# One-hot matrices built tile by tile from a scalar per edge, and counts by two products a pair, in a graph network kernel

## The chip, the cores and the metric

The kernel runs on one core of one Trainium2 chip. The metric is the time of one execution on the device in microseconds (us), the median of several runs; less is better. A core has five engines with an instruction queue each: TensorE (PE in the profile, its weight loads PEld), VectorE (DVE), ScalarE (ACT), GpSimd (POOL) and SyncE (SP, which only issues transfers here). All share a scratch memory of 128 partitions (SBUF); TensorE writes its results to PSUM.

## The reference

A graph network of three layers over 6250 nodes with 256 features and 100,000 edges of three types (relations). Edges are sorted by their target `dst`. Cut to what matters:

```
ew = edge_attr @ edge_w + edge_b                       # 100000 x 256
rel_masks = [(edge_type == i) for i in range(3)]
inv_cnt = [1 / max(segment_sum(m, dst), 1) for m in rel_masks]
for l in range(3):
    msg = relu(x[src] * ew)                            # a gather of 100000 rows
    out = 0
    for i in range(3):
        h = segment_sum(msg * rel_masks[i], dst) * inv_cnt[i]
        out += h @ weights[l, i]
    x = x + relu(out + x @ roots[l] + biases[l])
return layernorm(x_in + x)
```

All tensors are float32.

## The kernel before

The edges are cut into tiles of 128, one edge to a partition; two tiles make a *pair* (391 pairs), two pairs a *q* of four tiles. The layers' loop body `layer` walks through the pairs in a fixed `order` that is written out by hand (the scheduler is off: what the Python code says first stands first in each engine's queue). In step `it` of a layer it does the following.

- `gather` (line 900, in `gather_pair`) fetches the rows `x[src]` for the pair nine steps ahead: two indirect transfers on POOL's queue, one for each tile, each with 128 rows of 1 KB, into the tile `xs`. Behind the two stands `breath` (line 904): POOL fills 512 columns of a tile that nobody reads with zeros, a rest for the queue. The tiles `xs` of eight q can be in flight. The first six pairs of the next layer are gathered early, behind the last of this one.
- `reduce` (lines 641 to 647) makes the segment sums of the step's pair on TensorE: the rows `xs` as weights, the one-hot matrices `oh` as the moving side, two halves of the features by two tiles, each pair of products summed in PSUM (`h_p`).
- `make_ew` computes the edge weights `ew_p` in PSUM (lines 602 and 606), `add` (line 659) adds `h_p` to the running sums `acc` at a place that VectorE reads from a register.
- `weigh`, for the q three steps ahead, multiplies the rows by `ew_p` on VectorE (line 627) and takes Relu on ScalarE (line 629). VectorE waits here for the gathered rows to land.
- The node part: `root_turn` to `root_keep` (lines 664 to 677) and `node_mul`, `node_end` (lines 687 to 721) finish a chunk of 128 nodes every few steps, and write it to `x_mid`, from which the next layer gathers; the last layer's `norm` is line 738.
- `one_hot`, for the q two steps ahead, builds the matrices. Each edge has a number `seg` = 40 x type + distance of its target from the first target of its pair, and its row of the one-hot is 1 at that column of 120 (`WK`). One VectorE instruction (line 634) compares all four tiles: the counting row `iota_w` and `seg`, both stretched to 128 x 4 x 120.

In layer 0 alone the edges of each node and type are counted too. `one_hot` adds the two one-hots of a pair and rounds to bfloat16 (`oh_b`, line 638, VectorE), and `reduce` multiplies the sum by a matrix of ones (`full_ones`, line 647): one product a pair, into a third part of `h_p` (`CH` is 3 in layer 0 and 2 later; `DC` is 2).

A table `came` of comparisons with a scalar per partition is built once in layer 0 (line 568), by twelve instructions.

Of the kernel before, what the change touches and what calls it, by code (L numbers as in the profile page):

```python
# [9 lines left out]
BF = mybir.dt.bfloat16  # L10
I32 = mybir.dt.int32
AF = mybir.ActivationFunctionType
ALU = mybir.AluOpType
# [429 lines left out]
def ordered_path(ctx, tc, x, attr_laid, A, weights, roots, biases, edge_w, edge_b, out, src, src_i, seg, place_i, consts, x_root,  # L443
# [6 lines left out]
    nc = tc.nc  # L450
    P = 128
# [8 lines left out]
    DC = D // P  # L460
    WK = R * WIN
# [10 lines left out]
    ident, ones, iota_w = consts  # L472
# [40 lines left out]
    full_ones = big.tile([P, P], BF, name="full_ones")  # L513
# [15 lines left out]
    edge = ctx.enter_context(tc.tile_pool(name="edge", bufs=2))  # L529
# [40 lines left out]
    def layer(l, r_sb, b_sb, ats, early, pools):  # L570
# [7 lines left out]
        CH = DC + 1 if l == 0 else DC  # L578
        xs, ew_ps, ohs, h_ps, o_ps, rs = {}, {}, {}, {}, {}, {}
        x0s, mvs, oh_bs, t_ss, places = {}, {}, {}, {}, []  # L580
# [11 lines left out]
        def pairs_of(q):  # L592
            return range(min(2, U - 2 * q))
# [37 lines left out]
        def one_hot(q):  # L631
            ohs[q] = edge.tile([P, 4, WK], F32, name="oh", bufs=3)
            n = 2 * len(pairs_of(q))
            nc.vector.tensor_tensor(ohs[q][:, :n, :], iota_w[:, None, :].to_broadcast([P, n, WK]),  # L634
                                    seg[:, 4 * q:4 * q + n, None].to_broadcast([P, n, WK]), op=ALU.is_equal)
            if l == 0:
                oh_bs[q] = edge.tile([P, 2, WK], BF, name="oh_b", bufs=3)
                nc.vector.tensor_tensor(oh_bs[q][:, :n // 2], ohs[q][:, 0:n:2], ohs[q][:, 1:n:2], op=ALU.add)  # L638

        def reduce(u):  # L640
            h_ps[u] = h_pool.tile([P, DC + 1, WK], F32, name="h_p")
            for d in range(DC):
                for i in range(2):
                    nc.tensor.matmul(h_ps[u][:, d, :], xs[u // 2][:, u % 2, i, d * P:(d + 1) * P],  # L644
                                     ohs[u // 2][:, u % 2 * 2 + i, :], start=(i == 0), stop=(i == 1))
            if l == 0:
                nc.tensor.matmul(h_ps[u][:, DC, :], full_ones, oh_bs[u // 2][:, u % 2, :], start=True, stop=True)  # L647

        def add(u):
            if places[:1] != [u // 8]:  # L650
# [109 lines left out]
        for it in range(-11, max(starts) + 7):  # L760
# [21 lines left out]
            if pair(0) is not None:  # L782
                reduce(pair(0))
# [39 lines left out]
            if pair(2) is not None and first_of(it + 2, 2):  # L823
                one_hot(pair(2) // 2)
# [242 lines left out]
```

## Time and profile before

| | us |
|---|---|
| median of 3 runs | 3532.93 |
| lowest, highest | 3525.73, 3533.65 |
| the profiled execution | 3533.41 |
| its span in the profile | 3531.5 |

The span runs from the first instruction to the last. The mean granted TensorE clock was 0.86 of full speed. A group's row in the profile gives the line, the engine, the operation, the tile written and those read, the shapes, the number of instructions, then the time that the group was busy in us and the mean of one in ns, then the idle time of the engine just before them and what ended it ("issue" is a gap that no wait explains). A row of a line's own view gives the shortest, median and longest duration in ns. A row of the timeline gives the start and the duration in us, the engine, the line and, in brackets, the idle time before it. A row of the waits gives who waited for whom, the total in us, the times, and the longest.

### The profile page before, as it was taken

Reading aid. Unit: us, or ns where it says so; the run is one execution under the profiler, and the core shown is the slowest. Engines: PE = TensorE matmul, PEld = TensorE weight load, DVE = VectorE, ACT = ScalarE, POOL = GpSimd, SP = SyncE. Lnnn points to the kernel's source line nnn. Section 1 sums busy time; section 2 is a strip of 40 time slices with the busy share of each in tenths; the row PEclk is TensorE's granted clock in tenths of the full one; section 3 lists DMA queues with packets and bytes.
Section 4 is the critical chain, followed back from the end, with each engine's and each line's share of the span. In section 5 each row is a group of like instructions: output and inputs, shape, how many; then the busy total and the mean of one; then the engine's idle time right before and its main releaser. Section 6 shows DMA issues by size and latency. Waiting matters only on the chain.

```text
span 3531.5 us, 53355 instructions
## 1 busy us (share of the span) xinstructions
PE 2670.8 (76%) x18484; PEld 2212.9 (63%) x18484; DVE 2061.2 (58%) x4306; ACT 816.9 (23%) x959; POOL 2950.6 (84%) x3522
## 2 busy tenths in 40 slices
PE   5777777877787777777777777677787787777776
PEld 4666666666666566666666666556666666666655
DVE  6666666666765545555555555445555565666644
ACT  2222222222221122222222222112222222222221
POOL 7888888888888788888888888888888888888886
PEclk9888889998987888888889888778888888889877
DMA  5343433333333333333333333333334334333332
GB/s 161 107 119 115 124 106 106 108 106 111 112 111 106 106 102 102 103 105 107 104 108 107 110 111 113 106 105 111 115 113 115 107 112 115 113 109 111 111 100 82
DMA packets 173312, 387.75 MB, mean 110 GB/s; under 512 B 43418, under 2 KB 78636, under 8 KB 173036
## 3 DMA queue, kind: packets, MB, share of 16 engines
q0 software_dynamic: 112608, 307.65, 30.6%
q1 hardware_dynamic: 53136, 68.50, 6.2%
q10 hardware_dynamic: 7292, 8.11, 0.7%
q8 instruction: 151, 2.47, 0.3%
q14 instruction: 125, 1.02, 0.1%
HBM read 364.62 MB, written 19.46 MB: 109 GB/s over the span
## 4 chain that ended last, share of the span: by engine, by line
POOL 55%; issue 16%; PE 16%; DVE 6%; DMA 5%; POOLq 1%; ACT 0%; DVEq 0%; another core or an unknown queue 0%; ACTq 0%
POOL xs L900 43%; POOL breath L904 11%; PE h_p L644 7%; PE o_p L687 3%; DMA xs<-x_mid,src_io 3%; DVE xs L627 3%; PE ew_p L606 2%; DMA xs<-in_x_dram,src_io 1%; DVE acc L659 1%; PE r_p L672 1%; PE ew_p L602 1%; DVE x_root L718 1%; DVE oh L634 1%; POOLq L900 0%; PE h_p L647 0%
## 5 line engine op out<-in xcount | busy, mean ns | idle before, releaser
L900 POOL DMA_INDIRECT xs<-x_mid,src_io x1564 | 1544.9, 988 | 375.4 <-issue 359.0
L644 PE MATMUL h_p<-oh,xs 128*128 128x120 f32 x9336 | 1437.4, 308 | 350.7 <-DVE acc L659 230.4
L644 PEld LDWEIGHTS h_p<-oh,xs 128*128 128x128 f32 x9336 | 1335.8, 218 | 532.5 <-DVE acc L659 286.4
L627 DVE TENSOR_TENSOR xs<-ew_p,xs 128x512 f32<-128x512 f32 x1167 | 789.6, 687 | 1235.2 <-DMA xs<-x_mid,src_io 875.6
L629 ACT ACTIVATE xs<-xs 128x1024 f32<-128x1024 f32 (+1 forms) x588 | 617.7, 1051 | 2629.9 <-DVE xs L627 2369.1
L900 POOL DMA_INDIRECT xs<-in_x_dram,src_io x770 | 760.2, 987 | 180.9 <-issue 175.8
L904 POOL MEMSET breath<- 128x512 f32 x1167 | 634.8, 544 | 0.6
L659 DVE TENSOR_TENSOR acc<-h_p,acc 128x240 f32 (+1 forms) x1173 | 519.0, 442 | 108.6 <-PE o_p L687 30.4
L687 PE MATMUL o_p<-w_sb,acc 128*128 128x256 f32 (+1 forms) x1716 | 511.0, 441 | 76.4 <-DVE x_root L718 45.8
L606 PEld LDWEIGHTS ew_p<-ew_sb,at 32*128 32x128 f32 x4692 | 304.0, 225 | 319.3 <-issue 310.6
L602 PE MATMUL ew_p<-bias,full_ones 3*128 3x512 bf16 x1173 | 228.1, 419 | 329.4 <-DVE xs L627 274.9
L687 PEld LDWEIGHTS o_p<-w_sb,acc 128*128 128x128 f32 (+1 forms) x1716 | 355.4, 220 | 166.0 <-issue 39.4
L606 PE MATMUL ew_p<-ew_sb,at 32*128 32x256 f32 x4692 | 438.6, 469 | 3.7 <-issue 3.7
L634 DVE TENSOR_TENSOR oh<-iota_w,seg_o 128x480 f32<-128x480 f32 x588 | 381.2, 648 | 0.0
L672 PE MATMUL r_p<-r_sb,t_s 128*128 128x256 f32 x588 | 202.1, 477 | 76.6 <-ACT t_s L668 64.7
L718 DVE SCALAR_TENSOR_TENSOR x_root<-o_p,inv,x_root 128x256 f32<-128x256 f32 (+1 forms) x429 | 205.8, 480 | 34.3 <-PE o_p L687 15.5
L672 PEld LDWEIGHTS r_p<-r_sb,t_s 128*128 128x128 f32 x588 | 127.6, 241 | 101.0 <-ACT t_s L668 69.2
L704 ACT ACTIVATE acc<-zero_o 128x768 f32<-128x768 f32 (+1 forms) x150 | 140.3, 935 | 37.5 <-PE r_p L687 23.7
L602 PEld LDWEIGHTS <-full_ones 3*128 3x128 bf16 x1173 | 34.1, 92 | 139.1 <-issue 107.4
L647 PE MATMUL h_p<-oh_b,full_ones 128*128 128x120 bf16 x391 | 89.6, 229 | 0.1
L638 DVE TENSOR_TENSOR oh_b<-oh 128x240 bf16<-128x240 f32 x196 | 80.2, 409 | 6.7
L675 DVE TENSOR_TENSOR x_root<-r_p,b_sb 128x256 f32<-128x256 f32 x147 | 61.2, 416 | 8.6 <-PE r_p L672 2.7
(93 smaller groups left out, 564.0 us busy)
## 6 DMA issues: line engine op xcount, KB each, us to landing
at<-in_attr_laid_dram SPq DMA_DIRECT2D x147, 256.0 KB
xs<-x_mid,src_io POOLq DMA_INDIRECT x1564
xs<-in_x_dram,src_io POOLq DMA_INDIRECT x770
x_mid<-x_all SPq DMA_DIRECT2D x96, 128.0 KB
x_all<-in_x_dram ACTq DMA_DIRECT2D x8, 768.0 KB
x<-in_x_dram SPq DMA_DIRECT2D x48, 128.0 KB
out_dram<-x_all SPq DMA_DIRECT2D x48, 128.0 KB
w_sb<-in_L_gnn_weights_dram SPq DMA_DIRECT2D x3, 768.0 KB
```

Of the source, the lines that this page charges most:

```text
L602: nc.tensor.matmul(banks[j].rearrange("p i d -> p (i d)"), full_ones[j * A:j * A + PARTS, :], bias[j * A:j * A + PARTS].rearrange("p i d - ...
L606: nc.tensor.matmul(banks[j][:, i, :], ats[OCT * o // GROUP][j * A:(j + 1) * A, o % (GROUP // OCT), i, :], ew_sb[j * A:(j + 1) * A, :], sta ...
L627: nc.vector.tensor_mul(xs[q][:, k], ew_ps[2 * q + k], xs[q][:, k])
L629: nc.scalar.activation(there, there, AF.Relu)
L634: nc.vector.tensor_tensor(ohs[q][:, :n, :], iota_w[:, None, :].to_broadcast([P, n, WK]), seg[:, 4 * q:4 * q + n, None].to_broadcast([P, n, ...
L644: nc.tensor.matmul(h_ps[u][:, d, :], xs[u // 2][:, u % 2, i, d * P:(d + 1) * P], ohs[u // 2][:, u % 2 * 2 + i, :], start=(i == 0), stop=(i ...
L659: nc.vector.tensor_tensor(there, h_ps[u][:, :CH].rearrange("p c (r w) -> p c r w", r=R), there, op=ALU.add)
L672: nc.tensor.matmul(rs[c][:, 1, :], t_ss[c][:, d, :], r_sb[:, d, :], start=(d == 0), stop=(d == DC - 1))
L687: nc.tensor.matmul(o_p[:n, j, :], acc[:, d, r, slot:slot + n], w_sb[:, r * DC + d, :], start=(d == 0), stop=(d == DC - 1))
L718: nc.vector.scalar_tensor_tensor(root, o_p[:n, j, :], inv[:n, c, r:r + 1], root, op0=ALU.mult, op1=ALU.add)
L900: nc.gpsimd.indirect_dma_start(out=xs[:, u % 2, i, :], out_offset=None, in_=x_rows[:, :], in_offset=bass.IndirectOffsetOnAxis(ap=src_i[:, ...
L904: nc.gpsimd.memset(breath, 0.0)
```

## The change

`one_hot` no longer compares four tiles in one instruction with two stretched tensors. It issues one `tensor_scalar` for each tile: the row `iota_w` compared with one scalar per partition, the tile's column of `seg`. In layer 0 the four one-hots of a q are no longer summed by pairs on VectorE; ScalarE copies all four to bfloat16 (`oh_b` has four tiles now), and `reduce` counts by two products a pair with the matrix of ones, summed in PSUM as the others are. The gathers and `breath` stay as they are.

```diff
         def one_hot(q):
             ohs[q] = edge.tile([P, 4, WK], F32, name="oh", bufs=3)
             n = 2 * len(pairs_of(q))
-            nc.vector.tensor_tensor(ohs[q][:, :n, :], iota_w[:, None, :].to_broadcast([P, n, WK]),
-                                    seg[:, 4 * q:4 * q + n, None].to_broadcast([P, n, WK]), op=ALU.is_equal)
+            for t in range(n):
+                nc.vector.tensor_scalar(ohs[q][:, t, :], iota_w, seg[:, 4 * q + t:4 * q + t + 1], None,
+                                        op0=ALU.is_equal)
             if l == 0:
-                oh_bs[q] = edge.tile([P, 2, WK], BF, name="oh_b", bufs=3)
-                nc.vector.tensor_tensor(oh_bs[q][:, :n // 2], ohs[q][:, 0:n:2], ohs[q][:, 1:n:2], op=ALU.add)
+                oh_bs[q] = edge.tile([P, 4, WK], BF, name="oh_b", bufs=3)
+                nc.scalar.activation(oh_bs[q][:, :n], ohs[q][:, :n], AF.Copy)
 
         def reduce(u):
             h_ps[u] = h_pool.tile([P, DC + 1, WK], F32, name="h_p")
-            for d in range(DC):
+            for d in range(CH):
                 for i in range(2):
-                    nc.tensor.matmul(h_ps[u][:, d, :], xs[u // 2][:, u % 2, i, d * P:(d + 1) * P],
-                                     ohs[u // 2][:, u % 2 * 2 + i, :], start=(i == 0), stop=(i == 1))
-            if l == 0:
-                nc.tensor.matmul(h_ps[u][:, DC, :], full_ones, oh_bs[u // 2][:, u % 2, :], start=True, stop=True)
+                    nc.tensor.matmul(h_ps[u][:, d, :],
+                                     xs[u // 2][:, u % 2, i, d * P:(d + 1) * P] if d < DC else full_ones,
+                                     (ohs if d < DC else oh_bs)[u // 2][:, u % 2 * 2 + i, :],
+                                     start=(i == 0), stop=(i == 1))
```

## The prediction

> **What bounds the kernel now.** I read the page first: busy times, the chain that ended last, and the groups of POOL.
>
> ```profile
> PE 2670.8 (76%) x18484; PEld 2212.9 (63%) x18484; DVE 2061.2 (58%) x4306; ACT 816.9 (23%) x959; POOL 2950.6 (84%) x3522
> ...
> POOL 55%; issue 16%; PE 16%; DVE 6%; DMA 5%; POOLq 1%; ACT 0%; DVEq 0%; another core or an unknown queue 0%; ACTq 0%
> ...
> L900 POOL DMA_INDIRECT xs<-x_mid,src_io x1564 | 1544.9, 988 | 375.4 <-issue 359.0
> L900 POOL DMA_INDIRECT xs<-in_x_dram,src_io x770 | 760.2, 987 | 180.9 <-issue 175.8
> L904 POOL MEMSET breath<- 128x512 f32 x1167 | 634.8, 544 | 0.6
> ```
>
> POOL is busy for 2950.6 us, and idle before its gathers for 375.4 + 180.9 = 556.3 us, nearly all of it "issue", the fixed gap between one instruction and the next. Together that is 3506.9 of 3531.5 us: POOL's queue is the kernel's length. The waits say whether anybody makes POOL wait, and for what the engines behind it wait:
>
> ```profile
> DVE xs L627 <- DMA xs<-x_mid,src_io: 875.6, 443, 6.2
> ...
> POOL xs L900 <- issue: 534.9, 2254, 0.3
> ...
> POOL xs L900 <- PE h_p L644: 8.4, 29, 3.8
> ...
> POOL xs L900 <- PE ew_p L606: 5.9, 8, 4.8
> ```
>
> No gap of "issue" is over 0.3 us, and the two larger groups that name another engine come to 14.3 us, of which 3.8 and 4.8 are single waits. VectorE meanwhile sits 875.6 us until gathered rows land. So the other engines follow POOL, and the time moves only as far as the change makes POOL's own instructions shorter or longer, as long as no other engine fills up. POOL's instructions are not touched by the change; the question is why some of them are long. The two L900 rows of the view of that line, and the timeline at two places, show it:
>
> ```profile
> L900 POOL DMA_INDIRECT xs<-x_mid,src_io x1564: 942/955/1648, 1170.8 to 3513.0; - x196
> L900 POOL DMA_INDIRECT xs<-in_x_dram,src_io x770: 942/955/1519, 21.6 to 1169.1; - x193
> ```
>
> ```profile
> 1018.78 0.95 POOL L900 DMA_INDIRECT xs<-in_x_dram,src_io  x1 [0.16 <-issue]
> ...
> 1019.25 0.65 DVE L634 TENSOR_TENSOR oh<-iota_w,seg_o 128x480 f32<-128x480 f32 x1
> ...
> 1026.06 1.52 POOL L900 DMA_INDIRECT xs<-in_x_dram,src_io  x1 [0.30 <-issue]
> 1026.11 0.65 DVE L634 TENSOR_TENSOR oh<-iota_w,seg_o 128x480 f32<-128x480 f32 x1
> ```
>
> A gather takes 955 ns at the median, and up to 1648. The one at 1018.78 was half done when the one-hot instruction L634 came, and kept its 0.95 us. The one at 1026.06 had only begun (0.05 us) when L634 started, and took 1.52: 0.57 us more, nearly the length of L634. So a gather that begins beside an L634 waits until it has been read through. All that such waits can cost is the gap between mean and median: 1564 x (988 - 955) + 770 x (987 - 955) ns = 51.6 + 24.6 = 76 us. That is the whole sum which the change can win on POOL.
>
> **What the change removes.** L634 and L638 read two SBUF tensors each (L638 is the sum of the two one-hots of a pair, layer 0 only). Three other lines do the same and stay:
>
> ```profile
> L634 DVE TENSOR_TENSOR oh<-iota_w,seg_o 128x480 f32<-128x480 f32 x585 | 380.1, 650 | 0.0
> L638 DVE TENSOR_TENSOR oh_b<-oh 128x240 bf16<-128x240 f32 x195 | 79.9, 410 | 6.7
> L721 DVE SCALAR_TENSOR_TENSOR x_all<-x_root,x_all 128x256 f32<-128x256 f32 x144 | 61.8, 429 | 5.0
> L675 DVE TENSOR_TENSOR x_root<-r_p,b_sb 128x256 f32<-128x256 f32 x147 | 61.2, 416 | 8.6 <-PE r_p L672 2.7 <-issue 2.6 <-PE h_p L647 0.8
> L677 DVE TENSOR_TENSOR x_all<-x_all,x 128x256 f32<-128x256 f32 x49 | 20.4, 416 | 0.0
> L634 DVE TENSOR_TENSOR oh<-iota_w,seg_o 128x240 f32<-128x240 f32 x3 | 1.2, 397 | 0.0
> ```
>
> The two forms of L634 give (650 - 397) / 240 = 1.054 ns a column, so the columns of L634 take 506 ns, those of L638 253, those of the 256-wide lines 270. The chance that a gather begins in such a stretch grows with its length, and so does the wait; the loss goes as count x length squared: 585 x 0.506² = 149.8, 195 x 0.253² = 12.5, and for the three that stay (144 + 147 + 49) x 0.270² = 24.8. (I count L675 among them though one input is a PSUM tile; without it the share would be larger.) The removed lines hold 162.3 of 187.1, 87% of the 76 us: **66 us** off. If gathers fell at random, one every 3531.5 / 2346 = 1.505 us (2334 above and twelve early ones), the loss would be 162.3 / (2 x 1.505) = 54 us; I keep 54 and 76 as the ends.
>
> **What it adds on VectorE.** Each L634 becomes four TENSOR_SCALAR of 128x120 with a scalar per partition: 585 x 4 + 3 x 2 = 2346 of them. The nearest rows are the twelve TENSOR_SCALAR of L568 (128x128, 4-byte, the same is_equal with a scalar per partition, back to back), and POOL beside them:
>
> ```profile
> 87.17 0.55 POOL L904 MEMSET breath<- 128x512 f32 x1
> 87.88 0.97 POOL L900 DMA_INDIRECT xs<-in_x_dram,src_io  x1 [0.17 <-issue]
> 88.82 3.09 DVE L568 TENSOR_SCALAR came<-came,node_i 128x128 f32<-128x128 int32 x12 [6.15 <-DMA came<-in_src_dram]
> 89.16 0.97 POOL L900 DMA_INDIRECT xs<-in_x_dram,src_io  x1 [0.31 <-issue]
> 90.13 0.57 POOL L904 MEMSET breath<- 128x512 f32 x1
> 90.86 1.00 POOL L900 DMA_INDIRECT xs<-in_x_dram,src_io  x1 [0.16 <-issue]
> ...
> 92.17 1.48 POOL L900 DMA_INDIRECT xs<-in_x_dram,src_io  x1 [0.31 <-issue]
> 92.18 0.64 DVE L634 TENSOR_TENSOR oh<-iota_w,seg_o 128x480 f32<-128x480 f32 x1
> ```
>
> ```profile
> L738 DVE TENSOR_SCALAR x_all<-x_all,mv x49: 411/475/923, 2492.0 to 3525.6; 128x256 f32<-128x256 f32 x48, 106x256 f32<-106x256 f32 x1
> ```
>
> ```profile
> L568 DVE TENSOR_SCALAR came<-came,node_i x12: 268/284/756, 88.8 to 91.5; 128x128 f32<-128x128 int32 x12
> ```
>
> Two things are to be seen. These forms do contend with POOL, but it is mostly VectorE that waits: L568 goes from 268 to 756 ns and the float32 L738 from 411 to 923. And POOL loses little: against 0.95 and 0.55 us the four POOL instructions that meet the twelve are 0.02 + 0.02 + 0.02 + 0.05 = 0.11 us longer, about 10 ns for one TENSOR_SCALAR, while the single L634 at 92.18 lengthens the next gather by 0.53. So 2346 x 10 ns = **23 us** on, with 0 as the lower end. A lock released after each short piece, in place of one held for 506 ns, is why I take the row of L568 and not a share of L634's price.
>
> The Trainium skill speaks against this change (SBUF — State Buffer, Who interferes with whom): a tensor_scalar in a two-port mode and a GpSimd instruction exclude each other for the whole instruction, which starves the generation of a gather's descriptors, while a tensor_tensor from SBUF takes only the read interface that, as the page infers, descriptor generation does not need. The trace disagrees with the second half (1.52 us behind L634), and on the first shows VectorE as the one that mostly waits; what the rule would give is the first rival below.
>
> For VectorE itself the chain of four costs, at L568's 3.09 / 12 = 0.258 us each, waits included, 1.03 us in place of 0.65: 588 x 0.38 = +223 us, less 80 us of L638, so 2204 us or 63% of the span. Queued behind it are the next sums (L659) and products (L627), but VectorE has the 875.6 us of waiting for landings above to take it up: on the path it is nothing. Without that cover the 143 us would count in full.
>
> **What it adds on ScalarE and TensorE,** in layer 0 only. ScalarE gets 196 copies of 128x480, TensorE 391 more count products of the kind of L647.
>
> ```profile
> L647 PE MATMUL h_p<-oh_b,full_ones 128*128 128x120 bf16 x391 | 89.6, 229 | 0.1
> ...
> L668 ACT ACTIVATE t_s<-r_p 128x256 f32<-128x256 f32 x147 | 53.8, 366 | 0.1
> ...
> L647 PEld LDWEIGHTS <-full_ones 128*128 128x128 bf16 x391 | 45.1, 115 | 0.1
> ...
> L629 ACT ACTIVATE xs<-xs 128x512 f32<-128x512 f32 x9 | 5.7, 630 | 17.9 <-DVE xs L627 15.0 <-DVE inv L714 2.9
> ```
>
> ```profile
> 30.00:1170.00 1140.00, 892.61 (x6450) 730.44 (x6451) 745.52 (x1522) 274.27 (x299) 960.43 (x1147) 0.88 0.39 113
> 1190.00:2350.00 1160.00, 871.06 (x5942) 728.51 (x5941) 600.37 (x1226) 257.34 (x300) 974.80 (x1165) 0.85 0.37 106
> ```
>
> The windows' columns after the length are PE, PEld, DVE, ACT and POOL, then the clock. In layer 0 (the first) PE goes from 892.6 by at least 391 x 0.115 = 45 us (the weights' load alone) and at most 391 x (0.229 + 0.115) = 135 us, to 82 to 90% of 1140 us. ScalarE's copy lies between 0.366 and 0.630 us: 72 to 123 us onto 274, at most 35%. The copy waits for the four TENSOR_SCALAR; behind it in ScalarE's queue stands the next Relu, which waits for a later landing anyway, and the products read the counts two steps later, some 5.8 us (two pairs of 2 x 0.95 + 0.30 + 0.54 + 0.17 = 2.91 us). Nothing of this is on the path while POOL paces. At the layers' ends it may be: there POOL waits for the last sums.
>
> ```profile
> 1187.53 0.54 POOL L904 MEMSET breath<- 128x512 f32 x1
> 1192.84 0.95 POOL L900 DMA_INDIRECT xs<-x_mid,src_io  x1 [4.78 <-PE ew_p L606]
> ```
>
> Two such waits and the kernel's tail, each longer by 0 to 1 us (0.38 of the chain, up to 0.63 of the copy): I take 1 us in all.
>
> **The sum** against the profiled execution's 3533.4 us (span 3531.5; the median of the runs is 3532.9, so the same): 3533 - 66 + 23 + 1 = **3491 us**.
>
> **The rivals.**
> *Each TENSOR_SCALAR shuts POOL out for its whole length.* Price: POOL starts three instructions in 2.91 us, one each 0.97; one that falls at random into 268 ns waits 134 on average, so 0.268² / (2 x 0.97) = 37 ns for each, 2346 x 37 = 87 us: 3533 - 66 + 87 + 1 = 3555 us, slower. It decides from 66 / 2346 = 28 ns a piece on. For it: L738 and L568 prove an exclusion. Against it: 10 ns a piece beside L568. Chance 0.13; it is what the skill's rule gives.
> *The new form costs POOL nothing and the whole excess goes:* 3533 - 76 = 3457 us. Against it: the three lines that stay, and the 1.00 us at 90.86. Chance 0.10.
> *The pieces stick to POOL's gaps,* because a piece held back by a gather goes off at its end, just ahead of the next POOL instruction: double the 23 us and the low gain, 3533 - 54 + 46 + 1 = 3526, and with a little more no change. Chance 0.07.
> *VectorE becomes the bound:* it would need all pieces at the 0.756 us of L568's worst, 588 x (3.02 - 0.65) = +1394 us on 2061, 97% of the span; then some 3600 us. L568's median is 284 ns. Chance 0.03.
>
> **How the numbers follow.** The forecast has 0.67. The range takes in its ends (54 to 76 of gain, 0 to 46 of cost) and the second and most of the third rival: 3457 to 3531 us. A measurement of this kernel can tell about 0.3%, 11 us. Faster by more: 0.67 + 0.10 = 0.77; within: 0.07; slower: 0.13 + 0.03 = 0.16.
>
> **What would show it.** Right: the gathers' mean falls from 988 to some 970 ns (66 - 23 us over 2334 is 18), with few above 1.2 us and none of those beside a one-hot; L904 rises by a few ns; the one-hot pieces' mean is well over their minimum; POOL still waits for nobody; PE stays under 90% in layer 0. Wrong: gathers or memsets that are longer wherever a one-hot piece runs, a median of L904 well over 544, or POOL gaps that name DVE or PE.

## The result and the profile after

The changed kernel takes 3468.05 us (median of 4 runs, 3465.08 to 3471.03) against 3530.41 us before (4 runs): a ratio of 0.9824, 95% interval 0.9807 to 0.9841. It is 62 us faster, under 2% but clear of the interval; 42 were forecast (3533 to 3491).

The page of the kernel after: engines, the chain that ended last, and the groups on POOL and of the new one-hot line. (Lines have moved by one: L901 is the gather, L905 the rest, L635 the one-hot, L645 all products of `reduce`.)

```profile
PE 2657.0 (77%) x18875; PEld 2208.7 (64%) x18875; DVE 2144.7 (62%) x5868; ACT 931.5 (27%) x1155; POOL 2885.6 (83%) x3522
...
POOL 72%; issue 14%; PE 6%; DMA 4%; DVE 2%; POOLq 1%; ACT 0%; DVEq 0%; ACTq 0%
...
L901 POOL DMA_INDIRECT xs<-x_mid,src_io x1564 | 1499.9, 959 | 374.5 <-issue 361.0
L901 POOL DMA_INDIRECT xs<-in_x_dram,src_io x770 | 738.3, 959 | 180.9 <-issue 178.4
L905 POOL MEMSET breath<- 128x512 f32 x1167 | 637.1, 546 | 0.4
L635 DVE TENSOR_SCALAR oh<-iota_w,seg_o 128x120 f32<-128x120 f32 x2346 | 591.5, 359 | 0.0
```

The span went from 3531.5 to 3466.1 us, 65.4 less. The two rows of the gathers went from 1544.9 + 760.2 to 1499.9 + 738.3 us: 66.9 less. The rests cost 2.3 us more (634.8 to 637.1), and POOL's gaps are the same (556.3 and 555.4). The whole difference is in the duration of gathers that the change does not touch. The same line's own views and one place in the timeline:

```profile
L901 POOL DMA_INDIRECT xs<-x_mid,src_io x1564: 942/952/1293, 1149.2 to 3446.8; - x196
L901 POOL DMA_INDIRECT xs<-in_x_dram,src_io x770: 942/952/1821, 21.5 to 1147.6; - x193
...
L905 POOL MEMSET breath<- x1167: 538/543/693, 24.0 to 3447.7; 128x512 f32 x195
...
L635 DVE TENSOR_SCALAR oh<-iota_w,seg_o x2346: 248/278/817, 34.5 to 3451.4; 128x120 f32<-128x120 f32 x196
```

```profile
1007.47 1.00 POOL L901 DMA_INDIRECT xs<-in_x_dram,src_io  x1 [0.30 <-issue]
1007.50 1.14 DVE L635 TENSOR_SCALAR oh<-iota_w,seg_o 128x120 f32<-128x120 f32 x4
...
1008.47 0.62 POOL L905 MEMSET breath<- 128x512 f32 x1
...
1009.26 0.95 POOL L901 DMA_INDIRECT xs<-in_x_dram,src_io  x1 [0.16 <-issue]
```

This is the place to set beside 1026.06 of before. A gather begins, and 0.03 us later the one-hots do. Before that cost POOL 0.57 us; now the gather takes 1.00 and the rest behind it 0.62, some 0.12 us together, and it is VectorE whose four pieces take 1.14 us. In the two later layers the longest gather is 1293 ns, not 1648, and a piece of L635 that takes 248 ns at the least takes up to 817. Layer 0's longest gather did not get shorter (1821 ns against 1519). Counted over the two traces, 127 gathers of 2334 took over 1.2 us before and 7 after; six of these 7 begin inside another VectorE instruction that reads two SBUF tensors and was not changed (L699 and L702, which move sums within `acc`, L722, L678), the longest inside L699.

The place at 1026.06 was not the usual one, though. Before the change, 34 gathers had L634 start within 0.1 us after them, and 32 of these lost nothing. The loss is that of gathers that begin while L634 is already reading:

```profile
1007.40 0.65 DVE L634 TENSOR_TENSOR oh<-iota_w,seg_o 128x480 f32<-128x480 f32 x1
...
1007.95 0.95 POOL L900 DMA_INDIRECT xs<-in_x_dram,src_io  x1 [0.30 <-issue]
...
1015.35 0.65 DVE L634 TENSOR_TENSOR oh<-iota_w,seg_o 128x480 f32<-128x480 f32 x1
1015.43 1.39 POOL L900 DMA_INDIRECT xs<-in_x_dram,src_io  x1 [0.16 <-issue]
```

The gather at 1015.43 begins 0.08 us behind L634's start and takes 0.44 us more; the one at 1007.95 begins 0.55 us behind it and loses nothing. The 506 ns of columns that the prediction worked out would leave 0.43 us to wait in the first case and nothing in the second. Over the whole trace, gathers that begin 0.1 to 0.2 us behind L634's start are 364 ns longer than the median on average, those at 0.4 to 0.5 us 75 ns, those at 0.50 to 0.65 us not at all. The 268 gathers that begin in L634's first 506 ns lose 65.0 us together, the 47 that begin in L638's first 253 ns 6.0 us: 71.0 of the 76 us.

The waits that name POOL or the landings, and the window of layer 0 (columns: length, then PE, PEld, DVE, ACT, POOL):

```profile
DVE xs L627 <- DMA xs<-x_mid,src_io: 757.3, 428, 5.2
POOL xs L901 <- issue: 539.4, 2283, 0.3
...
POOL xs L901 <- PE h_p L645: 4.4, 26, 0.3
POOL xs L901 <- DMA x_mid<-x_all: 3.9, 1, 3.9
...
POOL xs L901 <- PE o_p L620: 3.8, 1, 3.8
```

```profile
30.00:1150.00 1120.00, 896.17 (x6852) 749.91 (x6853) 718.57 (x1911) 389.42 (x495) 940.33 (x1148) 0.89 0.39 115
```

POOL still waits for nobody but at the layers' ends, and VectorE still waits 757.3 us for landings. With the new count products PE is busy for 80% of layer 0, ScalarE for 35%: neither is near the pace.

### The profile page after: what moved, and what is told of

It reads as the page before. It is cut to its first block, busy times and chain, and to the rows that moved or that the text cites. A ratio compares the mean times of both kernels' runs of the same rounds, so it can differ in the third digit from the quotient of the medians.

```text
span 3466.1 us, 56101 instructions
## 1 busy us (share of the span) xinstructions
PE 2657.0 (77%) x18875; PEld 2208.7 (64%) x18875; DVE 2144.7 (62%) x5868; ACT 931.5 (27%) x1155; POOL 2885.6 (83%) x3522
## 4 chain that ended last, share of the span: by engine, by line
POOL 72%; issue 14%; PE 6%; DMA 4%; DVE 2%; POOLq 1%; ACT 0%; DVEq 0%; ACTq 0%
POOL xs L901 56%; POOL breath L905 16%; PE h_p L645 3%; DMA xs<-x_mid,src_io 2%; PE o_p L688 2%; DMA xs<-in_x_dram,src_io 1%; PE ew_p L606 1%; DVE xs L627 1%; POOLq L901 1%; PE r_p L673 0%; PE ew_p L602 0%; DVE acc L660 0%; DVE oh L635 0%; DVE x_root L719 0%; PE r_p L688 0%
## 5 line engine op out<-in xcount | busy, mean ns | idle before, releaser
L901 POOL DMA_INDIRECT xs<-x_mid,src_io x1564 | 1499.9, 959 | 374.5 <-issue 361.0
L645 PE MATMUL h_p<-oh,xs 128*128 128x120 f32 x9336 | 1420.9, 305 | 332.1 <-DVE acc L660 239.8
L645 PEld LDWEIGHTS h_p<-oh,xs 128*128 128x128 f32 x9336 | 1312.8, 215 | 509.4 <-DVE acc L660 309.0
L627 DVE TENSOR_TENSOR xs<-ew_p,xs 128x512 f32<-128x512 f32 x1167 | 790.4, 687 | 1168.2 <-DMA xs<-x_mid,src_io 757.3
L901 POOL DMA_INDIRECT xs<-in_x_dram,src_io x770 | 738.3, 959 | 180.9 <-issue 178.4
L905 POOL MEMSET breath<- 128x512 f32 x1167 | 637.1, 546 | 0.4
L635 DVE TENSOR_SCALAR oh<-iota_w,seg_o 128x120 f32<-128x120 f32 x2346 | 591.5, 359 | 0.0
L688 PE MATMUL o_p<-w_sb,acc 128*128 128x256 f32 (+1 forms) x1716 | 498.5, 433 | 67.2 <-DVE x_root L719 38.7
L688 PEld LDWEIGHTS o_p<-w_sb,acc 128*128 128x128 f32 (+1 forms) x1716 | 346.5, 215 | 152.3 <-DVE acc L660 39.2
L639 ACT ACTIVATE oh_b<-oh 128x480 bf16<-128x480 f32 x196 | 117.9, 601 | 152.3 <-DVE oh L635 126.5
L645 PE MATMUL h_p<-oh_b,full_ones 128*128 128x120 bf16 x782 | 110.2, 225 | 0.0
L645 PEld LDWEIGHTS <-full_ones 128*128 128x128 bf16 x782 | 84.7, 108 | 3.7
```

The costliest lines, as they stand in the source:

```text
L627: nc.vector.tensor_mul(xs[q][:, k], ew_ps[2 * q + k], xs[q][:, k])
L635: nc.vector.tensor_scalar(ohs[q][:, t, :], iota_w, seg[:, 4 * q + t:4 * q + t + 1], None, op0=ALU.is_equal)
L688: nc.tensor.matmul(o_p[:n, j, :], acc[:, d, r, slot:slot + n], w_sb[:, r * DC + d, :], start=(d == 0), stop=(d == DC - 1))
L901: nc.gpsimd.indirect_dma_start(out=xs[:, u % 2, i, :], out_offset=None, in_=x_rows[:, :], in_offset=bass.IndirectOffsetOnAxis(ap=src_i[:, ...
L905: nc.gpsimd.memset(breath, 0.0)
```

## The experiments

The theory: a gather that begins while VectorE reads two SBUF tensors waits until that reading ends; a scalar piece costs POOL a few ns and VectorE the rest. Rivals: the gain comes from moving the counts; the form of the instruction (tensor or scalar) is irrelevant and only its length counts; the pieces' price is higher than it looks. Each run's ratio is to the kernel before in the same comparison. In these comparisons the kernel before came out between 3525 and 3530 us, so differences of some 5 us between medians of different comparisons say little.

**The scalar pieces alone.** Counts as before; set against the kernel before, the edit is this.

```diff
-            nc.vector.tensor_tensor(ohs[q][:, :n, :], iota_w[:, None, :].to_broadcast([P, n, WK]),
-                                    seg[:, 4 * q:4 * q + n, None].to_broadcast([P, n, WK]), op=ALU.is_equal)
+            for t in range(n):
+                nc.vector.tensor_scalar(ohs[q][:, t, :], iota_w, seg[:, 4 * q + t:4 * q + t + 1], None,
+                                        op0=ALU.is_equal)
             if l == 0:
                 oh_bs[q] = edge.tile([P, 2, WK], BF, name="oh_b", bufs=3)
                 nc.vector.tensor_tensor(oh_bs[q][:, :n // 2], ohs[q][:, 0:n:2], ohs[q][:, 1:n:2], op=ALU.add)
```

> The one-hots by a scalar, tile by tile, but the counts as before (sum of two one-hots on VectorE, one product a pair). Theory (a gather that begins while a VectorE instruction reads two SBUF tensors waits for the end of that reading; the scalar pieces cost POOL some 5 ns each): all of the gain but the counts' sum's share, 6 to 7 us: about 3475 us, L900's mean near 962 ns. Rival (the gain is mostly the counts' move): 3500 us or more.

Measured: 3475.46 us, ratio 0.9854 (0.9839 to 0.9869), as the theory had it.

**The counts alone.** One-hots as before; set against the changed kernel, as the following edits are (the very last run's is set against the kernel before).

```diff
-            for t in range(n):
-                nc.vector.tensor_scalar(ohs[q][:, t, :], iota_w, seg[:, 4 * q + t:4 * q + t + 1], None,
-                                        op0=ALU.is_equal)
+            nc.vector.tensor_tensor(ohs[q][:, :n, :], iota_w[:, None, :].to_broadcast([P, n, WK]),
+                                    seg[:, 4 * q:4 * q + n, None].to_broadcast([P, n, WK]), op=ALU.is_equal)
             if l == 0:
                 oh_bs[q] = edge.tile([P, 4, WK], BF, name="oh_b", bufs=3)
                 nc.scalar.activation(oh_bs[q][:, :n], ohs[q][:, :n], AF.Copy)
```

> The counts moved (copy on ScalarE, two products a pair), but the one-hots in one instruction with two stretched tensors, as before. Theory: only the sum's share goes, 6 us of 3530: 3524 us, gathers still up to 1.5 us beside the one-hots. Rival (the counts' move is the gain): 3475 to 3500 us.

Measured: 3524.00 us against 3527.01, ratio 0.9992 (0.9983 to 1.0001). The gathers of the two runs, by groups, first the scalar pieces alone, then the counts alone:

```profile
L901 POOL DMA_INDIRECT xs<-x_mid,src_io x1564 | 1498.1, 958 | 374.6 <-issue 360.1 <-ACT xs L629 4.3 <-PE ew_p L606 3.7
L901 POOL DMA_INDIRECT xs<-in_x_dram,src_io x770 | 746.7, 970 | 180.9 <-issue 177.8 <-PE h_p L648 2.3 <-PE o_p L692 0.5
```

```profile
L900 POOL DMA_INDIRECT xs<-x_mid,src_io x1564 | 1541.3, 985 | 374.6 <-issue 362.5 <-PE h_p L644 5.6 <-DMA x_mid<-x_all 3.9
L900 POOL DMA_INDIRECT xs<-in_x_dram,src_io x770 | 751.1, 975 | 181.0 <-issue 176.9 <-PE h_p L644 1.6 <-ACT oh_b L638 0.5
```

The second row of each is layer 0, the only one that counts. With the old sum on VectorE its gathers have a mean of 970 ns where the later layers have 958; with the sum moved and the old one-hots layer 0 keeps 975 and the later layers 985. The pieces are the gain; the counts' move is worth 7 us between the medians of the first run and the changed kernel (3475 and 3468), 8 in their gathers of layer 0 (746.7 and 738.3), and 0 to 6 by its own comparison.

**Four pieces of two tensors.** The same cut, but each piece stays a comparison of two SBUF tensors.

```diff
-                nc.vector.tensor_scalar(ohs[q][:, t, :], iota_w, seg[:, 4 * q + t:4 * q + t + 1], None,
-                                        op0=ALU.is_equal)
+                nc.vector.tensor_tensor(ohs[q][:, t, :], iota_w,
+                                        seg[:, 4 * q + t:4 * q + t + 1].to_broadcast([P, WK]), op=ALU.is_equal)
```

> As the changed kernel, but each of the four pieces compares two tensors (128x120 each, seg stretched) in place of a tensor and a scalar. Theory in its first form (what counts is how long one reading holds: loss goes as count x length squared, 4 x 126 squared against 506 squared, a quarter of 66 us): 16 us in place of the 9 us that the gathers lose beside the scalar pieces, so about 3475 us. Rival (the four in a row hold POOL off as one, the form of the instruction is what counts): 3468 - 9 + 66 = 3525 us or more.

Measured: 3475.51 us, ratio 0.9858 (0.9843 to 0.9873).

```profile
L901 POOL DMA_INDIRECT xs<-x_mid,src_io x1564 | 1504.1, 962 | 374.6 <-issue 362.2 <-ACT xs L629 4.4 <-DMA x_mid<-x_all 3.8
L901 POOL DMA_INDIRECT xs<-in_x_dram,src_io x770 | 740.7, 962 | 181.0 <-issue 175.4 <-PE h_p L645 3.3 <-ACT oh_b L639 1.5
L905 POOL MEMSET breath<- 128x512 f32 x1167 | 633.9, 543 | 0.4
L635 DVE TENSOR_TENSOR oh<-iota_w,seg_o 128x120 f32<-128x120 f32 x2346 | 504.4, 276 | 0.0
```

Cutting alone brings nearly all of the gain, as the theory had it, so it is the length of one reading that counts: the rival that only length matters is true as far as it goes, and POOL does get in between the pieces. What the scalar form adds is a change of who pays. Two-tensor pieces keep VectorE busy for 504.4 us and leave the rests at 633.9 us, but the gathers lose 6.6 us more (2244.8 against 2238.2); scalar pieces keep it busy for 591.5 us, single ones for up to 817 ns where no two-tensor piece takes over 349, and lengthen the rests (637.1). Gathers and rests together differ by 3 us; the 7 us between the medians are from different comparisons.

**No one-hots on VectorE.** ScalarE takes the absolute difference per tile, then 1 minus it, cut at zero. (`minus` is the negative of `seg`, made once; `one` holds 1.)

```diff
-                nc.vector.tensor_scalar(ohs[q][:, t, :], iota_w, seg[:, 4 * q + t:4 * q + t + 1], None,
-                                        op0=ALU.is_equal)
+                nc.scalar.activation(ohs[q][:, t, :], iota_w, AF.Abs, bias=minus[:, 4 * q + t:4 * q + t + 1])
+            nc.scalar.activation(ohs[q][:, :n], ohs[q][:, :n], AF.Relu, bias=one, scale=-1.0)
```

> The one-hots on ScalarE (four times the absolute difference of the counting row and seg, then 1 minus that, cut at zero, for all four in one instruction); VectorE does nothing for them. Theory (what is left of the pieces' price on POOL is 9 us beside gathers and 2 us in the rests): 3468 - 11 = 3457 us. Rival (ScalarE's queue, with 588 x about 1.5 us more on it and the Relu behind it, takes the pace): above 3468 us, with POOL waiting for others.

Measured: 3458.27 us, ratio 0.9805 (0.9791 to 0.9818), as the theory had it.

```profile
L905 POOL DMA_INDIRECT xs<-x_mid,src_io x1564 | 1492.7, 954 | 374.8 <-issue 351.5 <-PE h_p L649 7.9 <-ACT oh L640 7.6
L905 POOL DMA_INDIRECT xs<-in_x_dram,src_io x770 | 734.6, 954 | 181.1 <-issue 167.9 <-ACT oh L640 4.1 <-ACT oh_b L643 3.1
L909 POOL MEMSET breath<- 128x512 f32 x1167 | 633.7, 543 | 0.4
```

This run splits the result into its two terms. Without any of the old or new one-hots on VectorE the kernel is 1.95% or 69 us below before: that is the gain. What the changed kernel has more is the price of the scalar pieces: 10.9 us on gathers (2238.2 less 2227.3) and 3.4 on rests (637.1 less 633.7) in the two profiles, 9.8 us between the medians.

**Each piece twice.** Once into a spare tile that nobody reads.

```diff
-                nc.vector.tensor_scalar(ohs[q][:, t, :], iota_w, seg[:, 4 * q + t:4 * q + t + 1], None,
-                                        op0=ALU.is_equal)
+                for there in (spare, ohs[q]):
+                    nc.vector.tensor_scalar(there[:, t, :], iota_w, seg[:, 4 * q + t:4 * q + t + 1], None,
+                                            op0=ALU.is_equal)
```

> Each of the 2346 scalar pieces is issued twice, once into a spare tile that nobody reads. Theory (5 ns of POOL a piece, as the changed kernel's gathers and rests show): 3468 + 12 = 3480 us. As the prediction had it (10 ns): 3491 us. A lock for the whole length of each piece (37 ns): 3555 us. VectorE's busy time rises to some 2700 us of it, 78%, and POOL still waits for nobody.

Measured: 3494.91 us, ratio 0.9916 (0.9903 to 0.9930). The 5 ns of the expectation were too few, and 37 are refuted.

```profile
L903 POOL DMA_INDIRECT xs<-x_mid,src_io x1564 | 1512.6, 967 | 374.0 <-issue 360.1 <-PE h_p L647 7.3 <-ACT xs L630 4.3
L903 POOL DMA_INDIRECT xs<-in_x_dram,src_io x770 | 744.7, 967 | 180.7 <-issue 175.9 <-PE h_p L647 2.5 <-ACT oh_b L641 1.2
L907 POOL MEMSET breath<- 128x512 f32 x1167 | 641.7, 550 | 0.5
```

POOL pays 19.1 us more on gathers (2257.3 less 2238.2) and 4.6 on rests for another 2346 pieces: 10.1 ns each, where the first 2346 cost (10.9 + 3.4) / 2346 = 6.1. But the median gather of this execution is 955 ns, not 952, and 3 ns in 2334 gathers are 7 us that need not be the pieces' doing (see the gain of 66 us below); without them it is 7.1 ns each. So the added pieces cost 7 to 10 ns, and that eight in a row are dearer for each than four is likely, not shown. The other 6 us between the two spans (3495.4 and 3466.1) lie behind the start of the last gather: 26.1 us are left there, 19.3 in the changed kernel.

**Rests of 256 columns.**

```diff
-    breath = big.tile([P, 512], F32, name="breath")
+    breath = big.tile([P, 256], F32, name="breath")
```

> The changed kernel with rests of 256 columns in place of 512. Theory (POOL's queue alone paces the kernel): each rest falls from 546 to about 279 ns, 1167 x 267 ns = 311 us off 3468: 3157 us, with PE at 84%. Rival (with the pace raised another engine, the granted clock or the landing of gathers takes over): well above 3157 us, with POOL waiting on PE or VectorE, and perhaps longer gathers.

Measured: 3210.18 us, ratio 0.9109 (0.9097 to 0.9122).

```profile
L901 POOL DMA_INDIRECT xs<-x_mid,src_io x1564 | 1493.4, 955 | 374.5 <-issue 357.4 <-PE h_p L645 4.9 <-PE ew_p L606 4.1
L901 POOL DMA_INDIRECT xs<-in_x_dram,src_io x770 | 736.1, 956 | 180.7 <-issue 173.2 <-PE h_p L645 3.6 <-ACT oh_b L639 1.0
L905 POOL MEMSET breath<- 128x256 f32 x1167 | 388.7, 333 | 0.4
```

The expectation took half a rest for half its price; it is 333 ns, not 279, and so the 3157 us were missed by 53. The rests fell by 248.4 us, the gathers by 8.7, together 257 of the 258 us between the medians: POOL's queue is the pace, as the theory said.

**No rests,** with the one-hots on ScalarE, with the changed kernel, and with the kernel before.

```diff
-    if breath is not None:
-        nc.gpsimd.memset(breath, 0.0)
```

> The one-hots on ScalarE as in the run before, and no rests at all. If POOL's queue stays the pace: a pair takes 2 x 0.952 + 2 x 0.304 = 2.51 us in place of 2.91, 1167 x 0.40 = 467 us off 3458: 2991 us, PE busy near 88%. Rival (PE or VectorE takes over): above 3050 us, with POOL waiting for PE by name.

> The changed kernel without rests. If POOL paces and the scalar pieces cost what they cost beside rests (12 us more on the gathers than with the one-hots on ScalarE): 3003 us. If pieces that find fewer gaps in POOL's queue cost more (up to 37 ns each): up to 3080 us. Rival (PE or VectorE takes over): POOL waits for them by name.

> The kernel before without rests. If a gather's loss is only its chance of beginning while L634 or L638 reads: gathers begin each 1.26 us in place of 1.505, so the 72 us that the changed kernel won become 86: 2987 + 74 (72 less 9 to 12 of the pieces, times 1.2) = some 3060 us. Rival (without rests the gathers fall into step with VectorE, or another engine takes over): the difference from the changed kernel without rests is under 40 or over 100 us.

Measured: 2977.19 us, ratio 0.8447 (0.8432 to 0.8462); 2986.62 us, 0.8476 (0.8460 to 0.8493); 3029.72 us, 0.8589 (0.8566 to 0.8612); 2991, 3003 and some 3060 were expected. The gathers by groups, in this order:

```profile
L905 POOL DMA_INDIRECT xs<-x_mid,src_io x1564 | 1484.3, 949 | 484.5 <-issue 401.8 <-ACT oh L639 28.1 <-DMA xs<-x_mid,src_io 13.4
L905 POOL DMA_INDIRECT xs<-in_x_dram,src_io x770 | 730.7, 949 | 234.6 <-issue 194.4 <-DMA xs<-in_x_dram,src_io 8.5 <-PE h_p L649 7.9
```

```profile
L901 POOL DMA_INDIRECT xs<-x_mid,src_io x1564 | 1490.2, 953 | 484.6 <-issue 422.2 <-DMA xs<-x_mid,src_io 12.5 <-PE ew_p L606 11.3
L901 POOL DMA_INDIRECT xs<-in_x_dram,src_io x770 | 735.3, 955 | 234.6 <-issue 196.8 <-ACT oh_b L639 8.5 <-PE h_p L645 8.5
```

```profile
L900 POOL DMA_INDIRECT xs<-x_mid,src_io x1564 | 1516.6, 970 | 484.6 <-issue 417.4 <-PE ew_p L606 13.7 <-PE h_p L644 13.1
L900 POOL DMA_INDIRECT xs<-in_x_dram,src_io x770 | 753.7, 979 | 234.6 <-issue 204.2 <-DMA xs<-in_x_dram,src_io 7.6 <-PE h_p L647 7.0
```

The idle time is the same in all three (719 us), so they differ by their gathers alone: 2215.0, 2225.5 and 2270.3 us. The price of the pieces on gathers (10.5 us) is what it was beside rests (10.9). The fastest version is the one with the one-hots on ScalarE and no rests. POOL's queue still adds up to the span (2225.5 + 719.2 of 2985.1 us in the changed kernel), but the chain that ended last now runs through the other engines as well:

```profile
POOL 27%; PE 24%; DMA 20%; issue 18%; DVE 8%; ACT 2%; DVEq 0%; POOLq 0%; ACTq 0%
...
POOL xs L901 <- issue: 619.0, 2032, 0.3
...
POOL xs L901 <- PE h_p L645: 18.6, 61, 0.3
```

The gaps that name TensorE are no longer than those of issue, 0.3 us, so POOL paces even without rests, with the others close behind.

The last expectation missed: the changed form is worth 43 us without rests, not the 74 that one gets from the rate at which gathers begin, and not under 40 either, as its rival had it. The forecast's own formula for gathers at random gives 162.3 / (2 x 1.29) = 63 us of loss here; the rows show 2270.3 - 2215.0 = 55. With rests the same formula gives 54, and the runs 69. The traces show why: gathers spread evenly would begin in the first 506 ns of an L634 197 times with rests and 229 times without; they do so 268 and 215 times. So the loss also hangs on where in POOL's round VectorE's one-hots fall. How that phase comes about was not tried.

## Why the prediction was right

- **The bound.** Right: POOL's durations explain the difference to 0.1 us (66.9 - 2.3 + 0.9 against 65.4), and the runs with shorter rests and none confirm it.
- **The gain of 66 us.** Right in kind, and nearly in size: 69 us by the run without one-hots on VectorE. The two profiles give 77.8 on gathers (2305.1 less 2227.3); 7 us of that is the median gather's 955 to 952 ns in 2334 gathers. It isn't the change's doing: the old one-hots with the counts moved show 952 as well, doubled scalar pieces 955, and gathers beside which VectorE does nothing at all have the same two medians, 955 before and 952 after. The execution of before that was profiled also lies above its median. Its cause is open, and so a few of the 62 us may not be the change's.
- **Which instructions hold a gather.** The list of the lines that stay was off, and the share hardly. Gathers that begin within 0.25 us of the start of L721 or L677 are 154 and 182 ns longer than the median, those of L675, which reads a PSUM tile and an SBUF tile, not at all (14 gathers, 2 ns shorter); nor do L659, L627 and L718, each with one input in PSUM, hold any. L698 and L701, 21 additions within `acc` with both inputs in SBUF, were left out. With L675 out and these two in, the formula gives 90% of the 76 us, 68 in place of 66.
- **The share of the two lines.** The counts' sum was put at 12.5 of 162.3, or 5 us; between the first run and the changed kernel it is 7 to 8, and the 47 gathers held by L638 lose 6.0 in the trace of before.
- **The cost of 23 us on POOL.** This is the term that was mis-sized: 14 us in the profiles, 10 in the medians, 4 to 6 ns a piece in place of 10. The row was right and its reading was rough: the rows of the timeline have two digits, and 0.95 and 0.55 us were taken as the undisturbed times where the medians are 0.955 and 0.544. The gather at 87.88 was counted too, though it was over 0.03 us after L568 began. The three that do meet the twelve take 970, 568 and 1003 ns in the trace, 87 ns more than those medians: 7 ns a piece, some 17 us in place of 23. This error and that of the gain both made the forecast too slow; nothing cancelled.
- **The rivals.** A lock for the whole piece (37 ns each, 3555 us) fell, twice: at 2346 pieces and at 4692. The rival without any cost has its 3457 us in the run that takes the one-hots off VectorE (3458), not in the changed kernel. The rival of pieces that stick to POOL's gaps is there in part: 345 gathers begin within 0.15 us of a piece's start, where an even spread gives 237, but the cost stayed far below its 46 us. That a tensor_tensor does not hold up a gather, as the Trainium skill infers (SBUF — State Buffer, Who interferes with whom), is contradicted: without the one-hots on VectorE the kernel is 69 us shorter. Another rule of that section agrees: an instruction with two SBUF inputs contends with a GpSimd instruction that reads SBUF, not with one that only writes it. The rests (zero fills) stay at 633.9 us beside two-tensor pieces.
- **VectorE off the path.** Right. The pieces are busy 591.5 us where 588 x 1.03 = 606 were forecast, VectorE 2144.7 where 2204 were.
- **Layer 0.** PE at 80%, below the 82 to 90 forecast: the 391 added products did not count in full, since all 782 are busy for 110.2 us where the 391 of before were for 89.6. ScalarE at 35% (at most 35). The two waits at the layers' ends did not grow: they are 3.9 and 3.8 us, where 4.8 and 3.8 stood before.

## What to carry to other kernels

When a queue of gathers on GpSimd sets the time, look at the difference between the mean and the median gather: in this kernel nearly all of it was the price of what VectorE did beside it. On VectorE, cut long instructions that read two SBUF tensors into short ones, or give one of the tensors as a scalar per partition: each gather then waits for a short reading at most, and VectorE, which has time here, is busy longer (381.2 us with the one-hots whole, 504.4 and 591.5 in pieces). An instruction that is there only to hold a pacing queue back (the rests: 481 us between 3468 and 2987 here) should be measured without before its neighbours are tuned.

## What the runs showed of the hardware

A gather is held only at its start: the 60 gathers that had run for 0.3 to 0.5 us when L634 started are 2 ns longer than the median on average. What holds it is a VectorE instruction with both inputs in SBUF (L634, L638, L721, L677); those with one input in PSUM (L675, L659, L627, L718) do not.

Scalar pieces hold a gather as well, but briefly: the 345 gathers that begin within 0.15 us of a piece's start lose 25 ns on average and 121 at most, beside two-tensor pieces of the same size 57 on average. Beside scalar pieces VectorE loses more than GpSimd: GpSimd lost 6 ns a piece, VectorE's busy time grew by (591.5 - 504.4) / 2346 = 37 ns a piece against two-tensor pieces. (The means, 359 and 276 ns, differ by more, because the durations of neighbouring pieces overlap.) Most of this is lost to the rests: without them the pieces are busy for 516.4 us.

```profile
L635 DVE TENSOR_SCALAR oh<-iota_w,seg_o 128x120 f32<-128x120 f32 x2346 | 516.4, 298 | 0.0
```

A zero fill on GpSimd beside scalar pieces takes 543 ns at the median for 512 columns and 330 for 256, which makes 0.83 ns a column and 117 fixed.
